# Moving key projections of a context attention beside a selective scan, by way of DRAM

## The chip, the core and the metric

The kernel runs on one core of a Trainium2 chip. The metric is the time of one execution on the device, in microseconds (us); before the change it is 1704.65 us (median of three runs, 1704.19 to 1710.15). The core's engines each work through their own instructions in order: TensorE (PE in the profile; PEld is its weight load), VectorE (DVE), ScalarE (ACT), GpSimd (POOL), and SyncE (SP), which here only issues DMAs. SBUF is the on-chip memory, PSUM the banks that TensorE writes to; DRAM is the memory outside the core.

## The reference, cut to what matters

A residual stream `x` of 4 batches x 128 tokens x 128 channels passes through four layers of three blocks each. Two blocks matter here.

The second block of the first layer is a selective state-space block in two directions, with 256 inner channels and 16 states per channel:

```python
delta = softplus(dt @ dtp_w.T + dtp_b)
A = -exp(A_log)
def step(h, inp):                       # one step in time
    u_t, d_t, b_t, c_t = inp
    h = h * exp(d_t[:, :, None] * A) + (d_t * u_t)[:, :, None] * b_t[:, None, :]
    return h, einsum('bdn,bn->bd', h, c_t)
```

The first block of the second layer is a cross attention of the 128 queries of each batch over 2048 rows of a context `ctx` with 96 channels, with 12 heads of 64 channels, biases on queries, keys and values, and a padding mask:

```python
q = x @ Wq.T + bq; k = ctx @ Wk.T + bk; v = ctx @ Wv.T + bv
weights = softmax(q @ k.T / sqrt(64), masked); out = (weights @ v) @ Wo.T + bo
```

The keys depend on the context and on weights alone, not on `x`, so they can be computed at any time.

## The kernel before, in words

The blocks run one after the other (`BLOCKS`). Weights are loaded with SP one block ahead (`nxt`), into a pool of two buffers. Inside the big blocks the order of the instructions on every engine is the order in which the Python code emits them (`manual_schedule`). A tile is taken from a pool with a fixed number of buffers per tag; an instruction that writes a tile waits until the buffer's last user is done.

**`mamba`, the selective scan.** `project(d)` prepares direction `d` in steps: `inputs` (transposes into `pads`), `conv` (two convolutions `xi_ps`, eight passes each), `gate` (`z_ps`), `dbl` (`xdbl_ps`, the store of the rows of B and C to DRAM as `bc_rows`, then two `dt_ps`), `exps`, `sums`, and `delta` per half (the softplus). All of these take their PSUM banks from the tag `mm`, which has three. Then there are 16 groups `(d, g, half)`: 2 directions x 4 quarters of the states x 2 halves of the channels. For group `i` the loop emits:

- the steps of `project(1)` that `side` puts there (0: inputs, taps; 1: conv, gate; 2: dbl; 3: exps; 4: sums; 5: delta),
- `spread`: SP loads the rows of B and C for the next quarter from DRAM, spread over 128 partitions (`b_rows` L1315, `c_rows` L1317, 1 MB each, two buffers each),
- on DVE the scan of 128 x 2048 (L1372) and the product with C (L1374),
- `total(i - 1)`: on PE eight passes that add up the states of the group before (`y_ps` L1348),
- `inputs(i + 2)`: on ACT four exponentials into `dA` (L1333; two buffers in all, so they wait for scan `i`), on DVE the input of the scan (L1337) into a buffer of the tag `h`, which has four and which `total` frees.

**`ctx_attention(1)` / `attend_units`, the context attention.** The 96 key blocks are 4 batches x 6 groups of two heads x 4 blocks of 512 context rows. A unit is a batch and four heads (two groups), so there are 12 units, three per batch. Per unit there are 8 key blocks (`key_steps`: a matmul `k_ps` L563 from the context, transposed, as `ctxT`; ACT adds the bias and copies to `kT`, L568), 8 score steps (`score_steps`: two matmuls `s_ps` L613 and two DVE instructions L620 that add the mask and take maxima), 8 exponentials (L632), and 16 chunks of four transposes (`t_ps` L726), a copy (`pT`) and the product with the context (`av` L719). The order is written out by hand: key blocks and scores of unit 0, key blocks of unit 1, and then a loop over the units, in which the score steps of the next unit and the key blocks of the one after that are spread over the 16 chunks. `context(b)` loads `ctxT` and `ctx` of a batch with SP; `mask(b)` loads the mask with ACT's queue (`mw` L539) and prepares it on POOL (`maskb` L542). A key fills a `kT` buffer of 128 x 2048; there are three.

Of the kernel before, what the change touches and what calls it, by code (L numbers as in the profile page):

```python
# [9 lines left out]
F32 = mybir.dt.float32  # L10
# [3 lines left out]
AF = mybir.ActivationFunctionType  # L14
# [85 lines left out]
class _XA:  # L100


    def __init__(self, heads, d, values, biases):
        self.heads, self.d = heads, d
        self.rows = 64 if d > 32 else 32
        self.per = P // self.rows
        self.groups = heads // self.per
        self.values = values
        self.biases = biases
        self.at = _Pack()  # L110
        for n, w in [("q", self.groups * P), ("k", self.groups * P), ("v", C if values else self.groups * DC),
                     ("o", heads * C), ("bq", self.groups), ("bk", self.groups), ("bv", self.groups)]:
            self.at.add(n, w)


XA = {1: _XA(12, 64, False, True), 2: _XA(8, 64, False, False), 3: _XA(8, 16, True, True)}


# [16 lines left out]
def _xattn_layout(xa, wq, wk, wv, wo, bq=None, bk=None, bv=None):  # L135

    h, d, g, per, rows = xa.heads, xa.d, xa.groups, xa.per, xa.rows

    def padded(m):
        out = np.zeros((m.shape[0], g, per, rows), np.float32)  # L140
        out[..., :d] = m.reshape(m.shape[0], g, per, d)
        return out.reshape(m.shape[0], g * P)

    def down(m):
        return padded(m.T).T.reshape(g, P, -1).transpose(1, 0, 2)

    out = np.zeros((P, xa.at.width), np.float32)
    out[:, xa.at["q"]] = padded(wq)
    out[:DC, xa.at["k"]] = padded(wk)
    if xa.values:  # L150
        out[:DC, xa.at["v"]] = wv
        out[DC, xa.at["v"]] = bv
    else:
        out[:, xa.at["v"]] = down(wv.T).reshape(P, -1)
    o = np.zeros((per, rows, g, per, C), np.float32)
    wod = down(wo).reshape(per, rows, g, C)
    for j in range(per):
        o[j, :, :, j] = wod[j]
    out[:, xa.at["o"]] = o.reshape(P, -1)
    for n, v in (("bq", bq), ("bk", bk), ("bv", None if xa.values else bv)):  # L160
        if v is not None:
            out[:, xa.at[n]] = down(v[:, None])[:, :, 0]
    return out


def _layout(i):
# [54 lines left out]
        axis=1,  # L221
    )
    a["cwr"] = np.concatenate([w[:, 0].T.reshape(-1) for w in both("conv_w")])[None]
    a["dtp"] = np.concatenate([m.T for m in both("dtp_w")], axis=1)
    a["l0f"] = np.concatenate([i["L0_ffn_w1"], kchunks(i["L0_ffn_w2"])], axis=1)

    a["xa1"] = _xattn_layout(
# [51 lines left out]
class Net:  # L279
    def __init__(self, ctx, tc, A):  # L280
        self.tc, self.nc, self.A = tc, tc.nc, A
        nc = self.nc
        self.cp = ctx.enter_context(tc.tile_pool(name="const", bufs=1))
        self.wp = ctx.enter_context(tc.tile_pool(name="weights", bufs=2))
        self.st = ctx.enter_context(tc.tile_pool(name="stats", bufs=4))
        self.x = self.cp.tile([P, B, C], F32, name="x")
        nc.scalar.dma_start(self.x, A["x"].rearrange("b t c -> t b c"))
        consts = self.cp.tile([P, CONSTS.width], F32, name="consts")
        nc.scalar.dma_start(consts, A["consts"])
        self.k = lambda n: consts[:, CONSTS[n]]  # L290
        self.ident = self.k("ident")
        self.ones = self.cp.tile([P, P], F32, name="ones")
        nc.gpsimd.memset(self.ones, 1.0)
        self.eps = self.cp.tile([P, 4], F32, name="eps")
        nc.gpsimd.memset(self.eps[:, 2:3], -MAGIC)
        nc.gpsimd.memset(self.eps[:, 3:4], EPS * EPS)
        nc.gpsimd.memset(self.eps[:, 0:1], EPS)
        nc.gpsimd.memset(self.eps[:, 1:2], 0.00064)
        cols = self.cp.tile([P, COLS.width], F32, name="cols")
        self.col = lambda n: cols[:, COLS[n]]  # L300
        self._flip = 0
        self._w = {}
        self._rows = {}
        nc.scalar.dma_start(cols, A["cols"])
# [185 lines left out]
    def attend_units(self, es, n, w, qT, wo, sense, first):  # L490
# [26 lines left out]
        def context(b):  # L517
            if b in ctxs or b >= B:
                return ctxs.get(b)
            c = {}  # L520
            lo = b * S + first * P
            c["T"] = cx.tile([DC + 1, keys], F32, tag="cT", name="ctxT")
            nc.sync.dma_start(c["T"][:DC], self.A["ctxT"][:, lo : lo + keys])
            if xa.values:
                nc.gpsimd.memset(c["T"][DC : DC + 1], 1.0)
                c["v"] = cx.tile([P, nch * C + 16], F32, tag="cv", name="val", bufs=1 + ahead)
                nc.gpsimd.memset(c["v"][:, nch * C :], 0.0)
            else:
                c["c"] = cx.tile([P, nch, DC], F32, tag="cc", name="ctx", bufs=1 + ahead)
                nc.sync.dma_start(  # L530
                    c["c"], self.A["ctx"][lo : lo + keys].rearrange("(c p) d -> p c d", p=P))
            ctxs[b] = c
            return c

        def mask(b):
# [8 lines left out]
                    ALU.mult, ALU.add)  # L544
            return masks[b]

        def key_steps(u):

            b, ug = units[u]
# [3 lines left out]

            def key(gi, j):
                def run():
                    c = context(b)
                    if sense is not None and ug == 0 and gi == 0 and j == nkq - 1:
                        mask(b)
                    if j == 0:
                        kT[gi] = kp.tile([P, keys], F32, tag="kT", name="kT")  # L560
                    g = ug * upg + gi
                    ps = s_ps.tile([P, 512], F32, tag="s", name="k_ps")
                    nc.tensor.matmul(  # L563
                        ps, W("k")[:DC, g * P : (g + 1) * P], c["T"][:DC, j * 512 : (j + 1) * 512],
                        start=True, stop=True)
                    to = kT[gi][:, j * 512 : (j + 1) * 512]
                    if xa.biases:
                        nc.scalar.activation(to, ps, AF.Identity, bias=W("bk")[:, g : g + 1])  # L568
                    else:
                        nc.scalar.copy(to, ps)  # L570
                return run

            def val(j):
# [9 lines left out]
                return run  # L583

            for gi in range(upg):
                steps += [key(gi, j) for j in range(nkq)]
            if xa.values and ug == 0:
                steps += [val(j) for j in range(nkq)]
            return steps
# [562 lines left out]
    def mamba(self, nxt):  # L1152
# [4 lines left out]

        nc, tc = self.nc, self.tc
        w = self.load("mamba")
        dtp = self.load("dtp")  # L1160
        MW = 512 + 80 + 256
        G = 4
        nxt()
        with tc.manual_schedule(), ExitStack() as es:
# [6 lines left out]
            xn = one.tile([P, B, C], F32, name="xn")  # L1171
            wc = one.tile([P, 2, 4, 256], F32, name="wc")
            lp = es.enter_context(tc.tile_pool(name="mb3", bufs=2))
            cwr = lp.tile([P, 2, 4, 256], F32, tag="h", name="cwr", bufs=4)
            for d in range(2):
                nc.sync.dma_start(
                    cwr[:, d].rearrange("p k c -> p (k c)"),
# [30 lines left out]
            def project(d):  # L1208
# [73 lines left out]
                def sums():  # L1282
                    for half in range(2):
# [2 lines left out]
                        nc.vector.tensor_scalar(q["r"], s["mm"][half], bias(half), 0.0, ALU.add, ALU.max)  # L1286
                        q["s"] = wk.tile([P, N], F32, tag="sp_s", name="sp_s")
                        nc.vector.tensor_scalar_add(q["s"], q["e"], 1.0)
                        q["l"] = wk.tile([P, N], F32, tag="sp_l", name="sp_l")
                        nc.scalar.activation(q["l"], q["s"], AF.Ln)  # L1290
                    if d == 0:
                        nc.vector.tensor_scalar_mul(A, A, -1.0)

                def delta(half):
                    q = sp[half]
                    nc.vector.scalar_tensor_tensor(q["e"], q["s"], -1.0, q["e"], ALU.add, ALU.subtract)
                    nc.vector.tensor_sub(q["r"], q["r"], q["e"])
                    dl = wk.tile([P, N], F32, tag=f"delta{half}", name="delta")
                    nc.vector.tensor_add(dl, q["r"], q["l"])
                    du = wk.tile([P, N], F32, tag=f"du{half}", name="du")  # L1300
                    nc.vector.tensor_mul(du, dl, s["u"][half])
                    s["delta"].append(dl)
                    s["du"].append(du)
                    s["y"] = []

                return [inputs, conv, gate, dbl, exps, sums, lambda: delta(0), lambda: delta(1)]

            groups = [(d, g, half) for d in range(2) for g in range(G) for half in range(2)]
            rows = {}
# [12 lines left out]
            def inputs(i):  # L1322
# [8 lines left out]
                for n in range(4):  # L1331
# [1 line left out]
                    nc.scalar.activation(  # L1333
                        dA[:, n, :, 1:], s["delta"][half].rearrange("p (b t) -> p b t", b=B)[:, :, 1:],
                        AF.Exp, scale=A[:, c : c + 1])
                dbu = lp.tile([P, 4, N], F32, tag="h", name="h", bufs=4)
                nc.vector.tensor_mul(dbu, bc_mid(s["du"][half], 4), rows[d, g][0])  # L1337
                dbus[i] = dbu

# [25 lines left out]
            for i, (d, g, half) in enumerate(groups):  # L1365
# [10 lines left out]
                if i:  # L1376
                    total(i - 1, hcs.pop(i - 1))
                inputs(i + 2)
            total(len(groups) - 1, hcs.pop(len(groups) - 1))
            out = ops.tile([P, B, C], F32, name="out_ps")  # L1380
            for b in range(B):
# [798 lines left out]
class _Doubled:  # L2180
# [14 lines left out]
    ("ctx_attention", (3, "bo3")), ("causal_attention", ()), ("routed_ffn", ()),  # L2195
]
WEIGHTS = [
    ("l0x",), ("mamba", "dtp"), ("l0f",), ("xa1",), ("r7",), ("moe1",),
    ("xa2",), ("l2a",), ("l2f",), ("xa3",), ("l3a",), ("l3f",),
]  # L2200

# [27 lines left out]
```

## Time and profile before

The profiled execution took 1707.17 us by the clock of the runs; its span, from the first to the last instruction, is 1705.3 us.

| stage | us of the span | what the busy time shows (us of the stage) |
|---|---|---|
| first layer's bit attention, start of the scan block | 0 to 211 | mixed |
| first direction's steps up to the first scan | 211 to 227 | DVE 12.9, ACT 13.2 of 16 |
| the 16 scan groups | 227 to 376 | DVE 146.6, PE 95.9, ACT 47.6 of 149 |
| end of the scan block, grouped feed-forward | 376 to 412 | PE 24.0 of 36 |
| queries of the context attention | 412 to 431 | PE 12.4 of 19 |
| context attention, before its loop | 431 to 465 | mixed |
| context attention, units 0 to 10 and their side work | 465 to 881 | PE nearly without gaps |
| the other eight blocks | 907 to 1705 | not touched but for the third context attention |

The whole execution has PE busy 79% of the span, DVE 58%, ACT 41%, POOL 2%, and the DMA engines move 31 GB/s on the mean. The page and the answers of the trace are read as follows. A line of a group gives line, engine, operation, the tile written and the tiles read; a line in order of time begins with its start and its duration, and what stands in brackets is how long the engine was idle before it and what it waited for. A table by stage gives the length, then the busy time of each engine with the number of instructions, the granted clock of TensorE as a share of its full speed, the share of the DMA engines and GB/s. Matmuls are pipelined, so the shown duration of one is longer than the distance to the next: the distance between two starts is what a pass costs.

### The profile page before, as it was taken

To read this page: it belongs to the slowest core of one execution; us is meant where nothing else is said; L and a number is where in the kernel's file an instruction comes from. 1 tells how busy PE (TensorE), PEld (TensorE's weight loads), DVE (VectorE), ACT (ScalarE), POOL (GpSimd) and SP (SyncE) were. 2 spreads that over 40 slices of the span, in tenths; PEclk is the share of its full clock that TensorE was granted. 3 is DMA by queue.
4 is the path that set the end of the run, shared out by engine and by line. 5 is a ranking of instruction groups with operands and counts; after the bars stand their busy time and mean duration, and the time that the engine had idled before them with its cause. 6 is when DMAs were issued, how large, how long until landed. Compare 5 with 4: busy or idle time off the path is not lost.

```text
span 1705.3 us, 17314 instructions
## 1 busy us (share of the span) xinstructions
PE 1343.3 (79%) x6385; PEld 706.7 (41%) x6387; DVE 991.2 (58%) x2334; ACT 707.6 (41%) x1237; POOL 40.5 (2%) x53
## 2 busy tenths in 40 slices
PE   1478665577799999999995677698968358999987
PEld 0145322234344444444441356473535225455444
DVE  6775499982244445444545877513548644566645
ACT  4653363213544554554432510234524213566642
POOL 0000000000000000000000000000002000000000
PEclk9978777788899999999996775699989556999998
DMA  4000143201300000000100000102000110000010
GB/s 138 0 1 1 30 177 118 98 29 68 80 19 7 19 19 7 19 7 1 42 9 29 1 1 1 50 0 69 18 13 1 48 39 19 20 1 1 2 49 7
DMA packets 21317, 53.57 MB, mean 31 GB/s; under 512 B 12052, under 2 KB 14748, under 8 KB 17000
## 3 DMA queue, kind: packets, MB, share of 16 engines
q1 hardware_dynamic: 17120, 46.55, 8.4%
q10 hardware_dynamic: 4104, 5.82, 1.1%
q8 instruction: 53, 0.87, 0.2%
q14 instruction: 40, 0.33, 0.1%
HBM read 51.97 MB, written 0.39 MB: 31 GB/s over the span
## 4 chain that ended last, share of the span: by engine, by line
PE 60%; DVE 24%; ACT 7%; issue 5%; DMA 2%; POOL 0%; DVEq 0%; ACTq 0%; POOLq 0%; SPq 0%
PE av L719 12%; PE s_ps L613 9%; PE t_ps L726 9%; PE k_ps L563 7%; DVE h L1372 4%; DVE p L620 3%; DVE h L1337 2%; PE av L715 2%; PE h_ps L1932 2%; PE y_ps L1939 2%; PE y L660 1%; PE o_ps L2005 1%; PE s_ps L977 1%; ACT wm L1665 1%; ACT p L632 1%
## 5 line engine op out<-in xcount | busy, mean ns | idle before, releaser
L340 DVE COPY pT<-t_ps 128x512 f32<-128x512 f32 x192 | 132.4, 690 | 219.3 <-PE t_ps L726 207.1
L632 ACT ACTIVATE p<-p,nm 128x1024 f32<-128x1024 f32 (+1 forms) x192 | 206.0, 1073 | 105.2 <-DVE nm L625 105.2
L719 PE MATMUL av<-pT,ctx 128*96 128x512 f32 x448 | 232.3, 606 | 1.0 <-ACT pT L338 1.0
L726 PEld LDWEIGHTS t_ps<-consts,p 128*128 128x128 f32 x1408 | 164.8, 141 | 154.8 <-issue 118.1
L726 PE MATMUL t_ps<-consts,p 128*128 128x128 f32 x1408 | 219.5, 279 | 0.0
L620 DVE CUSTOM_DVE_ANT_0 p<-s_ps,maskb 128x512 f32<-128x512 f32 x224 | 145.2, 688 | 112.1 <-PE s_ps L613 85.7
L338 ACT COPY pT<-t_ps 128x512 f32<-128x512 f32 x192 | 111.8, 582 | 229.7 <-PE t_ps L726 191.8
L613 PE MATMUL s_ps<-kT,qT 64*128 64x512 f32 (+1 forms) x704 | 181.1, 685 | 7.6 <-ACT kT L568 4.8
L563 PE MATMUL k_ps<-ctxT,w_xa 96*128 96x512 f32 x288 | 158.4, 650 | 17.9 <-DMA ctxT<-in_ctxT 14.7
L1348 PE MATMUL y_ps<-h,consts 128*128 128x512 f32 x128 | 80.1, 784 | 51.8 <-DVE h L1374 51.8
L568 ACT ACTIVATE kT<-k_ps,w_xa 128x512 f32<-128x512 f32 x128 | 87.3, 687 | 69.9 <-PE k_ps L563 69.9
L719 PEld LDWEIGHTS av<-pT,ctx 128*96 128x96 f32 x448 | 64.2, 162 | 112.3 <-issue 96.9
L620 DVE CUSTOM_DVE_ANT_0 p<-s_ps,zero 128x512 f32<-128x512 f32 x128 | 80.8, 687 | 37.1 <-PE s_ps L613 37.0
L613 PEld LDWEIGHTS s_ps<-kT,qT 64*128 64x128 f32 (+1 forms) x704 | 58.6, 194 | 44.4 <-issue 15.6
L1333 ACT ACTIVATE dA<-delta,A 128x508 f32<-128x508 f32 x64 | 40.7, 707 | 82.0 <-DVE h L1372 80.4
L1348 PEld LDWEIGHTS y_ps<-h,consts 128*128 128x128 f32 x128 | 30.8, 252 | 100.8 <-DVE h L1374 63.5
L563 PEld LDWEIGHTS k_ps<-ctxT,w_xa 96*128 96x128 f32 x288 | 50.9, 210 | 48.4 <-issue 35.6
L1372 DVE TENSOR_TENSOR_SCAN h<-dA,h 128x2048 f32<-128x2048 f32 x16 | 70.7, 4417 | 0.0
L715 PE MATMUL av<-pT,val 128*32 128x128 f32 x1024 | 55.2, 289 | 13.6 <-DVE pT L340 12.6
L663 DVE SCALAR_TENSOR_TENSOR x<-y,r,x 128x128 f32<-128x128 f32 x112 | 39.3, 351 | 12.8 <-PE y L660 6.5
L715 PEld LDWEIGHTS av<-pT,val 128*32 128x32 f32 x1024 | 20.4, 109 | 63.3 <-DVE pT L340 32.2
L1689 PE MATMUL sap<-pr,consts 128*128 128x64 f32 x120 | 33.3, 380 | 14.4 <-DVE pr L1687 13.7
(518 smaller groups left out, 1806.3 us busy)
## 6 DMA issues: line engine op xcount, KB each, us to landing
ctxT<-in_ctxT SPq DMA_DIRECT2D x12, 768.0 KB, 5.7
b_rows<-bc_rows SPq DMA_DIRECT2D x8, 1024.0 KB, 5.6
c_rows<-bc_rows SPq DMA_DIRECT2D x8, 1024.0 KB, 5.2
w_moe<-in_moe SPq DMA_DIRECT2D x2, 2048.0 KB, 7.4
ctx<-in_ctx SPq DMA_DIRECT2D x4, 768.0 KB, 7.9
w_l3f<-in_l3f SPq DMA_DIRECT2D x1, 1920.0 KB, 7.5
w_xa<-in_xa SPq DMA_DIRECT2D x1, 1833.0 KB, 7.7
w_xa<-in_xa SPq DMA_DIRECT2D x1, 1222.0 KB, 5.3
```

Source lines behind the costliest of these rows:

```text
L338: self.nc.scalar.copy(out, in_)
L340: self.nc.vector.tensor_copy(out, in_)
L563: nc.tensor.matmul(ps, W("k")[:DC, g * P : (g + 1) * P], c["T"][:DC, j * 512 : (j + 1) * 512], start=True, stop=True)
L568: nc.scalar.activation(to, ps, AF.Identity, bias=W("bk")[:, g : g + 1])
L613: nc.tensor.matmul(ps, qT[at, g, b * T : (b + 1) * T], kT[at, j * 512 : (j + 1) * 512], start=True, stop=True)
L620: nc.vector.tensor_tensor_reduce(st["p"][h, j * 512 // hw][:, j * 512 % hw : j * 512 % hw + 512], ps, in1, 1.0, -3.0e38, ALU.add, ALU.max, ...
L632: nc.scalar.activation(t, t, AF.Exp, bias=nm[:, h : h + 1], accum_out=st["s"][:, h, k : k + 1])
L715: nc.tensor.matmul(av[32 * i : 32 * i + 32, 0:P], c["v"][:, ch * C + h * 16 : ch * C + h * 16 + 32], pT[:, i * P : (i + 1) * P], start=ch ...
L719: nc.tensor.matmul(av[:DC], c["c"][:, ch], pT, start=ch == 0, stop=ch == nch - 1)
L726: nc.tensor.transpose(tr[:, i * P : (i + 1) * P], t[:, at : at + P], self.ident)
L1348: nc.tensor.matmul(y, self.ident, hc[:, n], start=g == 0 and n == 0, stop=False)
L1372: nc.vector.tensor_tensor_scan(self.flat(h), dA.rearrange("p n b t -> p (n b t)"), self.flat(h), 0.0, ALU.mult, ALU.add)
```

## The change

60 of the 96 key blocks of the second layer's context attention are projected in the scan's loop. After `inputs(i + 2)` group `i` emits the blocks 60i/16 to 60(i+1)/16: a matmul into a bank of `mm`, an ACT copy into `key` (two buffers), a store with SP into a DRAM tile `keys{b}`. The weights for it (`w_key`, 97 rows) are loaded once with ACT's queue, the context in halves of a batch (`ctx_half`, 97 x 1024, two buffers) with SP, and POOL writes a row of ones. The order of the blocks is batch, half, group, block of the half.

In `key_steps` the function `ready` says how many blocks of a key are there already; if there are any, SP loads them from DRAM into `kT` in one DMA, and their steps are left out. The bias of the keys is now a 97th row of their weights, met by a row of ones below `ctxT`, in the second and the fourth layer; ACT copies without a bias. The tag `h` has three buffers instead of four, the logarithm of the softplus is written in place (with the DVE instruction that reads its argument moved ahead of it), and `dtp` becomes a part of the weights `mamba` (256 KB wider, zeros below its 8 rows).

```diff
+HOISTED = 60
+    if bk is not None:
+        out[DC, xa.at["k"]] = padded(bk[None])[0]
...
+    a["mamba"] = np.concatenate([a["mamba"], np.concatenate([dtp, np.zeros((P - 8, dtp.shape[1]), np.float32)])], axis=1)
...
+            if xa.biases:
+                nc.gpsimd.memset(c["T"][DC : DC + 1], 1.0)
...
+        nk = DC + 1 if xa.biases else DC
+        def ready(b, nkq):
+            return max(0, min(4, 2 * ((HOISTED - b * 48) // 24))) if n == 1 else 0
...
                     if j == 0:
                         kT[gi] = kp.tile([P, keys], F32, tag="kT", name="kT")
+                        if ready(b, nkq):
+                            nc.sync.dma_start(kT[gi][:, : ready(b, nkq) * 512], self.hoisted[b][g, :, : ready(b, nkq) * 512])
+                    if j < ready(b, nkq):
+                        return
+                    c = context(b)
                     ps = s_ps.tile([P, 512], F32, tag="s", name="k_ps")
                     nc.tensor.matmul(
-                        ps, W("k")[:DC, g * P : (g + 1) * P], c["T"][:DC, j * 512 : (j + 1) * 512],
+                        ps, W("k")[:nk, g * P : (g + 1) * P], c["T"][:nk, j * 512 : (j + 1) * 512],
                         start=True, stop=True)
-                    to = kT[gi][:, j * 512 : (j + 1) * 512]
-                    if xa.biases:
-                        nc.scalar.activation(to, ps, AF.Identity, bias=W("bk")[:, g : g + 1])
-                    else:
-                        nc.scalar.copy(to, ps)
+                    nc.scalar.copy(kT[gi][:, j * 512 : (j + 1) * 512], ps)
...
-                steps += [key(gi, j) for j in range(nkq)]
+                steps += [key(gi, j) for j in range(nkq) if j == 0 or j >= ready(b, nkq)]
...
-            cwr = lp.tile([P, 2, 4, 256], F32, tag="h", name="cwr", bufs=4)
+            cwr = lp.tile([P, 2, 4, 256], F32, tag="h", name="cwr", bufs=3)
...
-                        q["l"] = wk.tile([P, N], F32, tag="sp_l", name="sp_l")
-                        nc.scalar.activation(q["l"], q["s"], AF.Ln)
+                        nc.vector.scalar_tensor_tensor(q["e"], q["s"], -1.0, q["e"], ALU.add, ALU.subtract)
+                        nc.scalar.activation(q["s"], q["s"], AF.Ln)
...
+            kp = es.enter_context(tc.tile_pool(name="mb_k", bufs=2))
+            xa = XA[1]
+            wkey = kp.tile([DC + 1, xa.groups * P], F32, name="w_key", bufs=1)
+            nc.scalar.dma_start(wkey, self.A["xa1"][: DC + 1, xa.at["k"]])
+            order = [(b, hf, g, j) for b in range(B) for hf in range(2) for g in range(xa.groups) for j in range(2)]
+            cts = {}
+            def ctx_half(b, hf):
+                if (b, hf) not in cts and order.index((b, hf, 0, 0)) < HOISTED:
+                    t = cts[b, hf] = kp.tile([DC + 1, 1024], F32, tag="ct", name="ctx_half")
+                    lo = b * S + hf * 1024
+                    nc.sync.dma_start(t[:DC], self.A["ctxT"][:, lo : lo + 1024])
+                    nc.gpsimd.memset(t[DC : DC + 1], 1.0)
+            def key(n):
+                b, hf, g, j = order[n]
+                if b not in self.hoisted:
+                    self.hoisted[b] = self.dram.tile([xa.groups, P, S], F32, name=f"keys{b}")
+                ctx_half(b, hf)
+                mm = ps.tile([P, N], F32, tag="mm", name="key_ps")
+                nc.tensor.matmul(
+                    mm, wkey[:, g * P : (g + 1) * P], cts[b, hf][:, j * 512 : (j + 1) * 512], start=True, stop=True)
+                t = kp.tile([P, N], F32, tag="key", name="key", bufs=2)
+                nc.scalar.copy(t, mm)
+                lo = hf * 1024 + j * 512
+                nc.sync.dma_start(self.hoisted[b][g, :, lo : lo + 512], t)
...
                 inputs(i + 2)
+                for n in range(HOISTED * i // 16, HOISTED * (i + 1) // 16):
+                    key(n)
```

## The prediction

> **What bounds the kernel now.** I read the chain of work that ended last first, then the busy time by stage, then the waits and order of time in the two stages that the diff touches.
>
> ```profile
> PE 60%; DVE 24%; ACT 7%; issue 5%; DMA 2%; POOL 0%; DVEq 0%; ACTq 0%; POOLq 0%; SPq 0%
> ```
>
> Busy time by stage (columns named in its first line):
>
> ```profile
> core 0: us, PE busy (x) PEld busy (x) DVE busy (x) ACT busy (x) POOL busy (x), PEclk, DMA share, GB/s
> 227.00:376.00 149.00, 95.86 (x159) 37.27 (x160) 146.57 (x62) 47.60 (x71) 0.00 (x0) 0.80 0.25 92
> 447.00:846.00 399.00, 395.87 (x1540) 184.83 (x1539) 185.53 (x500) 203.50 (x348) 5.70 (x3) 0.99 0.04 10
> ```
>
> Two stages, two limits. The selective scan (227 to 376 us) has DVE busy 146.6 of 149 us: DVE sets its end, PE and ACT have holes. The second layer's context attention (447 to 846) has PE busy 395.9 of 399: every PE pass there is on the path. Work moved from the second to the first pays if it truly fits the holes.
>
> ```profile
> ACT dA L1333 <- DVE h L1372: 80.4, 13, 12.1
> ...
> PE y_ps L1348 <- DVE h L1374: 49.7, 13, 8.4
> ```
>
> Those were the waits of 227 to 372 us (total, times, longest). DVE in order of time (start, duration):
>
> ```profile
> 240.80 2.29 DVE L1374 TENSOR_TENSOR h<-h,c_rows 128x2048 f32<-128x2048 f32 x1
> 243.01 2.28 DVE L1337 TENSOR_TENSOR h<-du,b_rows 128x2048 f32<-128x2048 f32 x1
> 245.21 4.42 DVE L1372 TENSOR_TENSOR_SCAN h<-dA,h 128x2048 f32<-128x2048 f32 x1
> ```
>
> One scan group is three DVE instructions back to back: scan 4.42, product 2.2, next input 2.2 (starts 2.2 apart), 8.86 us in all. ACT's exponentials (4 x 0.64 = 2.55) wait for the scan, PE's sums for the product. In such in-order queues a hole is free only if nothing due stands behind the filler.
>
> The start of the attention and a stretch of its first loop, in order of time:
>
> ```profile
> 437.23 0.33 ACTq L539 DMA_DIRECT2D mw<-in_mask  x1
> 441.29 1.90 POOL L542 TENSOR_SCALAR maskb<-mw 128x2048 bf16<-128x2048 uint8 x1 [35.81 <-DMA mw<-in_mask]
> 443.22 0.69 DVE L620 CUSTOM_DVE_ANT_0 p<-s_ps,maskb 128x512 f32<-128x512 f32 x1 [22.58 <-POOL maskb L542]
> ...
> 479.87 1.02 PE L563 MATMUL k_ps<-ctxT,w_xa 96*128 96x512 f32 x2
> 480.74 1.02 PE L719 MATMUL av<-pT,ctx 128*96 128x512 f32 x2
> ```
>
> In the attention a key block is two passes, 480.74 - 479.87 = 0.87 us of PE. Before its loop (first transposes at 465.16) DVE's first score work waits for the mask, whose DMA stands in ACT's queue behind key copies.
>
> **What the change really moves.** `HOISTED` is 60, and `order` has 24 blocks per batch (2 halves x 6 groups x 2). But `ready` computes 2 * ((60 - 48b) // 24), at most 4: batch 0 gets 4, batch 1 gets 2 * (12 // 24) = 0, later ones 0. So 60 blocks are projected and stored beside the scan, 24 are read, 72 are still projected in the attention, and 36 are done twice. I take this as read off the code.
>
> **Gain in the attention.** Batch 0 is units 0 to 2: 8 blocks each. Unit 2's stand in the loop of unit 0: 8 x 0.87 = 6.9 us of a bound PE. (The last unit, with no side steps at all, still runs PE without gaps at 1.30 us a chunk, so PE stays the limit.) Units 0 and 1 stand before the loop. With no key copies ahead of it, the mask's DMA leaves ACT right after the last query copy (425.93 + 0.69 = 426.6); 4.1 us to Pool's start as now and 1.9 on Pool give 432.7 instead of 443.2. Sixteen score rows at 0.61 and the third of four 1.14 us exponentials then end at 446.4, where unit 1's key blocks now keep PE until 465.16: 18.7 less. Against it stand a PE back at half clock for two chunks (1.5 us), and 1 to 2 us if the mask's 256 KB shares the engines with key loads. The key loads are 1 MB each on SP; a 1 MB row load alone lands in 4.6 us, so 425.96 + 4.6 = 430.6 is before the mask even at the latest start. `ctx` now queues behind four of them: about 448, when the first product needs it. I take 15.5 (13 to 18). Sum 22.4, from 18 to 25. Pool's new 1.8 us memsets have 100 us of idle Pool; copy instead of biased copy (0.59 for 0.69) is off the path.
>
> **Cost in the scan.** Each of 16 groups gets 3 or 4 blocks: two passes (0.43 each at full clock, 0.85 at half, both seen in one sum of eight), an ACT copy (0.59, as ACT's copies of 128x512 take), a 256 KB store on SP. I walked the queues instruction by instruction with these durations; the same walk without keys puts the last scan at 367.1, as the trace does. What came late:
> - Group 1. Three blocks of group 0 hold all three `mm` banks until their copies, which stand behind the exponentials of group 2: scan end 231.9 + 2.55 + 0.59 = 235.1. The second direction's convolution, now at 227.7, waits for that; the sum of group 0 behind it ends near 249.5 instead of 242.3. `h` has three buffers, one fewer, so the input of group 3 (243.0) waits for that sum: 6.5 us of DVE.
> - Group 2. The last copy of group 1 ends at 255.0 (it waits for earlier stores to land); `xdbl`'s copy and its small store come behind it, and SP reaches `b_rows` of the third quarter only at 256.6: it lands 4.6 later, 261.3, and DVE wanted it at 258.3: 3.0.
> - Groups 3 and 4. `dt_ps` holds two banks until `sums` in group 4, so blocks 7 to 14 share one: matmul, copy, matmul, with the sums behind them on PE: 0.3. The last of these stores leaves at 281.7, `b_rows` of the fourth quarter behind it lands at 286.5, DVE wanted it at 283.0: 3.5.
> - Groups 6, 8, 10, 12, where DVE needs the next quarter. The copies begin at scan end + 2.55; the third waits for the first store (two `key` buffers; the kernel's own 256 KB store of `out` took 2.3 us), so the fourth store leaves 7.1 after the scan. `b_rows`, which SP now issues behind it (today as soon as its buffer is free), lands 4.6 later with 0.6 of queue between: 12.3. DVE wants it after product, input, scan and product, 2.2 + 2.2 + 4.4 + 2.2 = 11.1. So 1.2 in groups 10 and 12; 2.1 in group 6, where both row loads wait behind the stores; none in group 8, whose predecessor has a `yT` product (0.7) more.
> - After the last product the last sum (8 passes and 2) stands behind four blocks: 3.3.
>
> Together 6.5 + 3.0 + 0.3 + 3.5 + 2.1 + 2.4 + 3.3 = 21.1, taken as 21. With stores at 1.6 us (the 64 KB store's row) the walk gives 18, with 0.5 us more per loaded MB 25; I keep 15 to 28. The softplus edit moves two 0.68 us DVE steps and removes none: 0. Folding `dtp` into the first weight load adds 256 KB to the start, where the DMA engines are full at about 300 GB/s: 0.7 us (0 to 1).
>
> A rule speaks against the stores: the Trainium skill, DMA: Bandwidth & Descriptors, Anatomy of one DMA, says that about 2 us of every DMA are fixed, mostly the receipt of the last write, longest when the target is HBM. Its fit (2.0 us plus bytes over 436 GB/s) would make an estimated 2.6 us of each store, 0.3 above the row; by it the walk's cost would be about 22 instead of 21.
>
> **Sum.** The profiled execution took 1707.2 us (span 1705.3, 1.9 around it), 2.5 above the median of the runs. 1707.2 + 21 + 0.7 - 22.4 = 1706.5; on the median's scale 1704.0. The walk knows no wait that the code does not show, and such waits only add, so I take 1 more: 1705.
>
> **Rivals.**
> - The row loads fall well behind the key stores (slower). The place is SP's queue: `b_rows` has no slack once the last store of the group before leaves later than 11.1 - 4.6 = 6.5 us after the scan, and every further us is paid by DVE at six row loads. If stores wait for each other (they write one DRAM tile in interleaved rows), the fourth leaves at 3.3 + 3 x 2.3 = 10.2, 3 us later than I took: 6 x 3 = 18 us, 1723; with the early groups longer too, 1730. For it: SP had nothing but loads here, and one wrong wait repeats. Against: the stores write separate bytes.
> - The fillers really hide (faster). PE has 53 us of idle time and ACT 101 in the scan. If the convolution gets its bank in time and row loads are issued early, what is left is the tail of 3.3 and perhaps 3: 1705 - 15 = 1690. Against it: three `mm` banks, and program order on SP.
> - All 60 blocks are used: 36 x 0.87 = 31 us more, 1674. The arithmetic of `ready` excludes it.
>
> **How the numbers follow.** A measurement of this kernel can tell about 0.5%, 8.5 us, from no change. Gain and cost nearly cancel, by bounds from 1705 - 9 to 1705 + 10: chance 0.45, nearly all within 0.5%. Slow row loads 0.32, 1713 to 1730 and over. Hidden fillers 0.22, 1685 to 1696. All 60 used: 0.01. The range reaches to the ends of both neighbours: 1689 to 1730; the likeliest case alone has 1696 to 1715. Faster 0.23, same 0.45, slower 0.32.
>
> **What would show it.** Right: 60 `key` copies and stores in the scan, `k_ps` 48 instructions fewer in the attention, first transposes 15 to 19 us sooner after the last query copy, unit 0's loop 30.5 instead of 37.4 us, the last scan about 18 us later, DVE waiting before L1337's line for a `y_ps` sum early and for `b_rows` in even groups. Wrong: DVE still without gaps in the scan (the second rival), SP waiting for DMA before key stores (the first), or attention units of batch 1 without `k_ps` (the third).

## The result, and the profile after

The changed kernel takes 1720.6 us (median of six runs, 1716.6 to 1725.7) beside 1708.6 us for the kernel before on the same chip: a ratio of 1.0076, 95% interval 1.0052 to 1.0099. It is slower by some 13 us, just past what can be told from no change. The profiled execution has a span of 1720.8 us, 15.5 more than before. All places below are from such profiled executions.

The chain of work that ended last, by engine, on the page after:

```profile
PE 61%; DVE 20%; ACT 8%; issue 4%; DMA 4%; POOL 1%; SPq 0%; DVEq 0%; ACTq 0%; POOLq 0%
```

DVE gave up 4 points and DMA won 2: transfers now stand in the chain. Busy time by stage, the scan first and then the attention's loop:

```profile
core 0: us, PE busy (x) PEld busy (x) DVE busy (x) ACT busy (x) POOL busy (x), PEclk, DMA share, GB/s
232.00:404.00 172.00, 138.53 (x267) 55.67 (x266) 146.61 (x62) 78.32 (x127) 2.84 (x3) 0.85 0.48 168
470.00:862.00 392.00, 386.23 (x1515) 181.61 (x1516) 189.62 (x512) 187.19 (x332) 12.89 (x8) 0.98 0.09 27
```

DVE does the same 147 us of work in the scan, but the stage is 172 instead of 149 us long: DVE now stands idle for 25 us, while PE and ACT are fuller. The holes were filled and the bound engine paid. Its waits between 225 and 412 us:

```profile
engine line waited for: us in total, times, longest us
DVE h L1381 <- DMA b_rows<-bc_rows: 14.5, 5, 4.6
DVE h L1381 <- PE y_ps L1392: 9.4, 2, 6.5
DVE yT L1395 <- PE y_ps L1394: 7.7, 2, 7.0
```

(`yT` is the product with the gate that follows a sum of `y`.) All are new but 4.05 us of the last line. DVE in order of time, the first three groups:

```profile
241.25 4.42 DVE L1416 TENSOR_TENSOR_SCAN h<-dA,h 128x2048 f32<-128x2048 f32 x1
245.70 2.29 DVE L1418 TENSOR_TENSOR h<-h,c_rows 128x2048 f32<-128x2048 f32 x1
254.47 2.29 DVE L1381 TENSOR_TENSOR h<-du,b_rows 128x2048 f32<-128x2048 f32 x1 [6.48 <-PE y_ps L1392]
256.68 4.42 DVE L1416 TENSOR_TENSOR_SCAN h<-dA,h 128x2048 f32<-128x2048 f32 x1
261.13 2.29 DVE L1418 TENSOR_TENSOR h<-h,c_rows 128x2048 f32<-128x2048 f32 x1
268.00 2.29 DVE L1381 TENSOR_TENSOR h<-du,b_rows 128x2048 f32<-128x2048 f32 x1 [4.58 <-DMA b_rows<-bc_rows]
```

What were three instructions back to back now has a wait ahead of each third one: first for a sum of `y` (no free buffer of `h`), then for a row load. Ahead of that sum in PE's queue stands the convolution of the second direction, which has to wait for a bank until ACT has copied a key block out of one:

```profile
239.90 9.38 PE L1239 MATMUL xi_ps<-pad,wc 128*128 128x512 f32 x16 [3.59 <-ACT key L1344]
```

The start of the attention, in order of time:

```profile
464.81 0.34 ACTq L546 DMA_DIRECT2D mw<-in_mask  x1
468.15 1.90 POOL L549 TENSOR_SCALAR maskb<-mw 128x2048 bf16<-128x2048 uint8 x1 [23.94 <-DMA mw<-in_mask]
470.08 0.69 DVE L633 CUSTOM_DVE_ANT_0 p<-s_ps,maskb 128x512 f32<-128x512 f32 x1 [10.64 <-POOL maskb L549]
```

The mask leaves with the last query copy (464.73), and first score work comes 4.7 us after that copy's end instead of 16.6 before. The gain is there. `k_ps` has 48 instructions fewer: 24 blocks are read from DRAM and 60 were written.

Two places were not in the sum. The first is the start. ACT's long sum over `w_l0x` in order of time, before and after:

```profile
17.23 1.06 ACT L831 ACTIVATE junk<-w_l0x 128x1024 f32<-128x1024 f32 x1 [3.58 <-DMA w_l0x<-in_l0x]
```

```profile
21.67 1.06 ACT L844 ACTIVATE junk<-w_l0x 128x1024 f32<-128x1024 f32 x1 [5.17 <-DMA w_l0x<-in_l0x]
```

The second lies between the scan and the feed-forward. The load `ew` of 4 KB holds DVE (in order of time, before and after):

```profile
390.44 0.16 DVE L1405 TENSOR_REDUCE ews<-ew 128x4 f32<-128x8 f32 x1 [6.04 <-DMA ew<-in_ew]
```

```profile
417.12 0.36 DVE L360 BATCH_NORM_AGGREGATE ln_mv<-ln_st 128x2 f32<-128x6 f32 x4
428.66 0.16 DVE L1451 TENSOR_REDUCE ews<-ew 128x4 f32<-128x8 f32 x1 [11.18 <-DMA ew<-in_ew]
```

Its landing took 13.0 us (7.8 before). Three 1 MB key loads and `w_xa` leave SP at 412.3 to 416.8 and share the DMA engines with it; before, it was `w_xa` alone. In the traces' records of single packets, the 512 packets of `ew`, 8 bytes each, take 9.3 us from first to last instead of 3.9. The layer norm behind this reduction in DVE's queue, and so the first feed-forward matmul, wait too.

Where the 16.3 us at the end of the attention (906.62 to 922.96) come from:

| stretch | before | after | change |
|---|---|---|---|
| start to first scan | 227.5 | 232.4 | +4.9 |
| first scan to last `yT` | 151.0 | 179.2 | +28.2 |
| last `yT` to first `h_ps` (`ew`) | 16.6 | 21.8 | +5.2 |
| from there to the load `w_r`, which ends the feed-forward | 16.6 | 17.1 | +0.5 |
| `w_r` to the end of the attention | 494.9 | 472.5 | -22.5 |

### The profile page after: what moved, and what is told of

It is laid out like the page before. It is cut to its first block, busy times and chain, and to the rows that moved or that the text cites. A ratio compares the mean times of both kernels' runs of the same rounds, so it can differ in the third digit from the quotient of the medians.

```text
span 1720.8 us, 17714 instructions
## 1 busy us (share of the span) xinstructions
PE 1367.7 (79%) x6457; PEld 719.5 (42%) x6459; DVE 992.1 (58%) x2334; ACT 716.2 (42%) x1273; POOL 52.4 (3%) x62
## 4 chain that ended last, share of the span: by engine, by line
PE 61%; DVE 20%; ACT 8%; issue 4%; DMA 4%; POOL 1%; SPq 0%; DVEq 0%; ACTq 0%; POOLq 0%
PE av L732 12%; PE s_ps L626 10%; PE t_ps L739 9%; PE k_ps L580 6%; DVE p L633 3%; DVE h L1416 2%; PE av L728 2%; PE h_ps L1978 2%; PE y_ps L1985 2%; DMA b_rows<-bc_rows 1%; PE y_ps L1392 1%; PE y L673 1%; PE o_ps L2051 1%; PE xi_ps L1239 1%; DVE h L1381 1%
## 5 line engine op out<-in xcount | busy, mean ns | idle before, releaser
L580 PE MATMUL k_ps<-ctxT,w_xa 97*128 97x512 f32 (+1 forms) x240 | 130.3, 635 | 9.0 <-DMA ctxT<-in_ctxT 9.0
L583 ACT COPY kT<-k_ps 128x512 f32<-128x512 f32 x120 | 69.9, 585 | 71.4 <-PE k_ps L580 68.0
L1341 PE MATMUL key_ps<-ctx_half,w_key 97*128 97x512 f32 x120 | 64.8, 669 | 37.9 <-ACT key L1344 25.9
L1392 PE MATMUL y_ps<-h,consts 128*128 128x512 f32 x128 | 68.9, 689 | 2.2 <-DVE h L1418 2.2
L1344 ACT COPY key<-key_ps 128x512 f32<-128x512 f32 x60 | 34.1, 582 | 66.3 <-DMA keys<-key 42.1
L1341 PEld LDWEIGHTS key_ps<-ctx_half,w_key 97*128 97x128 f32 x120 | 23.4, 206 | 71.9 <-issue 38.5
L580 PEld LDWEIGHTS k_ps<-ctxT,w_xa 97*128 97x128 f32 (+1 forms) x240 | 40.5, 205 | 27.8 <-issue 21.9
L1381 DVE TENSOR_TENSOR h<-du,b_rows 128x2048 f32<-128x2048 f32 x16 | 36.6, 2288 | 23.9 <-DMA b_rows<-bc_rows 14.5
```

What stands on the lines that cost most here:

```text
L580: nc.tensor.matmul(ps, W("k")[:nk, g * P : (g + 1) * P], c["T"][:nk, j * 512 : (j + 1) * 512], start=True, stop=True)
L1341: nc.tensor.matmul(mm, wkey[:, g * P : (g + 1) * P], cts[b, hf][:, j * 512 : (j + 1) * 512], start=True, stop=True)
L1392: nc.tensor.matmul(y, self.ident, hc[:, n], start=g == 0 and n == 0, stop=False)
```

## The experiments

Each kernel ran beside the kernel before on the same chip, and each ratio is against that; kernels that ran on different chips are compared by their ratios. "Changed" is the changed kernel.

**Count the blocks in twelves**, so that all 60 are read (changed, one line):

```diff
-            return max(0, min(4, 2 * ((HOISTED - b * 48) // 24))) if n == 1 else 0
+            return max(0, min(4, 2 * ((HOISTED - b * 24) // 12))) if n == 1 else 0
```

> The changed kernel with the count in `ready` mended to 2 * ((60 - 24b) // 12), so that all 60 stored blocks are read (batches 0 and 1 whole, half of batch 2). Theory A (PE bounds the attention, a block there is two passes): 36 blocks fewer at 0.87 us, 31 us less than the changed kernel, about 1689 us, 0.989 of the kernel before; the 10 further key loads of 1 or 0.5 MB hide. Theory B (the loop of the attention falls back on key loads, or on DVE and ACT once the side steps are few): less than half of that, 1705 or more.

Measured: 1699.4 us, ratio 0.9934 (0.9910 to 0.9957). So `ready` did throw 36 blocks away, and with them read the change beats the kernel before. The gain over the changed kernel, 24 us by the ratios, lies between the two theories. From the first product to the end of the attention 406.9 us pass instead of 432.5, 25.6 less, not the 31 that 36 x 0.87 makes. By the distances of the units' output products, the three units with no key block at all saved 15.9 of 20.6 us, and three units with half of their blocks 9.7 of 10.3. The busy time of the first two of those units in this kernel, by windows:

```profile
core 0: us, PE busy (x) PEld busy (x) DVE busy (x) ACT busy (x) POOL busy (x), PEclk, DMA share, GB/s
523.00:555.00 32.00, 31.59 (x136) 14.80 (x135) 15.89 (x44) 13.74 (x24) 0.00 (x0) 1.00 0.21 75
555.00:590.00 35.00, 33.45 (x142) 15.87 (x142) 20.09 (x56) 14.12 (x25) 3.70 (x2) 1.00 0.17 61
```

PE has 0.4 and 1.5 us of holes there where it had none; the rest of the missing 5 us stays open.

**Project only the blocks that are read**: 24 projected, 24 read.

```diff
-HOISTED = 60
+HOISTED = 24
-            return max(0, min(4, 2 * ((HOISTED - b * 48) // 24))) if n == 1 else 0
+            return max(0, min(4, 2 * ((HOISTED - b * 24) // 12))) if n == 1 else 0
```

> Only 24 blocks are projected beside the scan, and the same number of blocks is read in the attention as in the changed kernel (here 8 for each of the first three units, counted by twelve). So the attention keeps its gain and only the fillers of the scan change: 24 instead of 60. Theory A (the cost is queueing: what a group can hide costs nothing, and the third and fourth block of a group make nearly all of the wait): first scan to last yT falls from 179.2 us to 153 to 157 (151.0 before the change), time 1694 to 1699. Theory B (each block costs the same, 28.2 / 60 = 0.47 us): 24 blocks cost 11 us, first scan to last yT 162, time about 1704.

Measured: 1696.0 us, ratio 0.9926 (0.9892 to 0.9959). First scan to last `yT` takes 154.0 us, 3.0 more than before the change: theory A. The 36 blocks that nobody reads cost 25 of the 28 us. In the whole scan one wait of DVE for an input is left, in order of time:

```profile
259.30 2.29 DVE L1381 TENSOR_TENSOR h<-du,b_rows 128x2048 f32<-128x2048 f32 x1 [2.01 <-PE y_ps L1392]
```

With three banks, and with the row loads behind the stores, one or two blocks per group fit into the holes; the third and fourth are what DVE pays for. That is no fixed limit: with both of these mended, 60 blocks cost 7.3 us (below, all mends at once).

**Row loads ahead of the key stores** in SP's queue (changed):

```diff
                 inputs(i + 2)
+                if half == 1:
+                    spread(*divmod(d * G + g + 2, G))
                 for n in range(HOISTED * i // 16, HOISTED * (i + 1) // 16):
```

> The changed kernel with the row loads of the next quarter issued one group earlier, ahead of that group's key stores on SP. Theory A (the row loads behind the stores are what DVE waits for): the 14.5 us of DVE waiting for b_rows go, and the time falls by 10 to 15 us, 1706 to 1711. Theory B (ACT and PE are late anyway and take over as the thing waited for): the time falls by less than 4 us.

Measured: 1710.1 us, ratio 1.0007 (0.9993 to 1.0020). First to last scan takes 151.5 us instead of 164.1, and first scan to last `yT` 164.2 instead of 179.2. No wait for `b_rows` is left in the loop; three for sums of `y` are, in order of time:

```profile
255.74 2.29 DVE L1381 TENSOR_TENSOR h<-du,b_rows 128x2048 f32<-128x2048 f32 x1 [6.56 <-PE y_ps L1392]
267.29 2.29 DVE L1381 TENSOR_TENSOR h<-du,b_rows 128x2048 f32<-128x2048 f32 x1 [2.60 <-PE y_ps L1392]
278.73 2.29 DVE L1381 TENSOR_TENSOR h<-du,b_rows 128x2048 f32<-128x2048 f32 x1 [2.49 <-PE y_ps L1392]
```

The order on SP, not the traffic of the stores, made the row loads late: the same 60 stores still run.

**Five `mm` banks** instead of three (changed):

```diff
-            ps = ... tc.tile_pool(name="mb_ps", bufs=3, space=PSUM)
-            yps = ... tc.tile_pool(name="mb_yps", bufs=4, space=PSUM)
+            ps = ... tc.tile_pool(name="mb_ps", bufs=5, space=PSUM)
+            yps = ... tc.tile_pool(name="mb_yps", bufs=2, space=PSUM)
```

> As the changed kernel, but with five `mm` banks of PSUM and two for the sums of y instead of three and four. Theory A (the early waits of DVE, 6.5 us in group 1 and what follows from it in groups 2 to 4, come from key blocks that hold all three `mm` banks until their copies): the 6.5 us wait for y_ps goes, and 8 to 12 us with its followers: 1708.5 to 1712.5. Theory B (the order of ACT's copies and of SP's stores sets these waits, and the banks only pass it on): the waits stay or move to b_rows, less than 4 us: 1717 or more.

Measured: 1712.8 us, ratio 1.0008 (0.9991 to 1.0024); first scan to last `yT` takes 168.9 us, 10.3 less. The size is that of theory A, at the edge of its range, but the wait did not simply go. DVE's waits in this stretch:

```profile
engine line waited for: us in total, times, longest us
DVE h L1381 <- DMA b_rows<-bc_rows: 8.7, 4, 3.7
DVE h L1381 <- PE y_ps L1392: 7.1, 1, 7.1
```

Group 1 has no wait any more and group 2 has one of 7.1 us for a sum of `y`. The banks let the early groups run on until the next shortage: PE then waits 2.3 us for the copy of `xdbl`, which stands on ACT behind four key copies, and these behind key stores. The edit also takes the banks of the sums from four to two; no wait of this stretch is put down to that.

One part of the change was never tried alone: the tag `h` has three buffers instead of four. With a fourth, the input of group 3 would not have to wait for the sum of group 0. So the waits for sums of `y` (9.4 us in the changed kernel) may be in part its price; no run tells.

**`dtp` in the load of the scan weights, alone** (kernel before, with this edit only):

```diff
-    a["dtp"] = np.concatenate([m.T for m in both("dtp_w")], axis=1)
+    dtp = np.concatenate([m.T for m in both("dtp_w")], axis=1)
+    a["mamba"] = np.concatenate([a["mamba"], np.concatenate([dtp, np.zeros((P - 8, dtp.shape[1]), np.float32)])], axis=1)
...
-        dtp = self.load("dtp")
+        dtp = w[:8, 2 * (512 + 80 + 256) :]
```

> The kernel before with one part of the change alone: `dtp` folded into the first weight load (256 KB wider). Theory A (the wider load displaces what the first block waits for): the second sum over the first block's weights starts some 4 us later than in the kernel before, as in the profile of the changed kernel, and the time is 3 to 5 us longer, 1712. Theory B (the 4 us at the start were chance; 256 KB cost what they take to move): under 1 us.

Measured: 1713.0 us, ratio 1.0019 (1.0006 to 1.0032). The long sum starts at 23.14 us (17.23 before), the first scan at 232.85, the attention ends 4.9 us later. The loss at the start is this edit's: in all kernels here that have it, with the weights in one transfer at their old place, the long sum starts at 21.7 to 23.1 us, in those without it at 17.2 to 17.5.

Two kernels ask why 256 KB cost so much. **The scan weights behind all of `ctxT`** (changed):

```diff
         w = self.load("l0x")
-        nxt()
...
                 nc.sync.dma_start(ctxT[:DC, at], self.A["ctxT"][:, at])
+            nxt()
```

> The changed kernel with the first scan weights (w_mamba, now 1,104 KB) loaded on SP's queue behind the four pieces of ctxT instead of behind the first. The same bytes in all. Theory A (bytes that stand ahead: w_l0x on ACT's queue is late because these 1,104 KB are moved before it): the second w_l0x sum, at 21.67 us in the changed kernel and 17.23 before, starts at 17 us or sooner, first scan 228 or sooner, time 4 to 5 us less than the changed kernel. Theory B (the two queues take turns packet by packet, and SP's queue has packets of 8 KB in either order, of ctxT or of the weights): the second sum stays at 20.5 to 23 us, time within 2 us of the changed kernel's.

**The scan weights in four pieces** (changed):

```diff
+            elif name == "mamba":
+                at = self.A[name].shape[1] // 4
+                for j in range(4):
+                    cols = slice(j * at, (j + 1) * at)
+                    self.nc.sync.dma_start(t[:, cols], self.A[name][:, cols])
```

> The changed kernel with the first scan weights loaded in four pieces of 276 KB (2.2 KB per partition row) at the same place of SP's queue. The same bytes in all, smaller packets. Theory B (turns packet by packet): while these pieces move, ACT's queue gets a larger share, and the second w_l0x sum starts at 15 to 18 us instead of 21.67, time 4 to 6 us less than the changed kernel. Theory A (bytes): it stays at 20.5 to 23 us and the time within 2 us of the changed kernel's.

Measured: 1721.0 us, ratio 1.0057 (1.0041 to 1.0074), for the first; 1717.9 us, ratio 1.0052 (1.0034 to 1.0071), for the second. Both intervals overlap that of the changed kernel, so the times do not tell the theories apart; the traces do. The long sum starts at 18.66 in the first, and in the second, in order of time:

```profile
13.76 1.04 ACT L849 ACTIVATE junk<-w_l0x 128x1024 f32<-128x1024 f32 x1
```

So smaller pieces of the same bytes give 7.9 us, past theory B's range, and 3.5 us more than was lost. The later place gives 3.0, which neither theory's range holds. Bytes that stand ahead do not explain it: with all mends (below) the same move takes 848 KB from ahead of `w_l0x`, and the long sum starts later, at 18.60 instead of 17.53.

The traces also record each packet with its queue and size, one per row of a load, and they show what `w_l0x` runs beside. Its own 128 packets (6 KB each) take, from the first start to the last end:

| kernel | `w_l0x` | packets of SP's queue meanwhile |
|---|---|---|
| before | 6.2 us | 122 of `ctxT`, 8 KB each |
| changed | 9.8 us | 209 of `ctxT` |
| `dtp` alone | 11.0 us | 240 of `ctxT` |
| weights later | 6.1 us | 116 of `ctxT` |
| weights in four | 2.7 us | 113 of the weights, 2.2 KB each |

In the changed kernel the weights' packets have ended when those of `w_l0x` begin. So it is not delayed by the wider rows beside it but by what follows them: more of `ctxT` goes beside it. Why 256 KB shift the two queues that far is not shown. The Trainium skill, DMA: Bandwidth & Descriptors, Queues, rings and completion order, states that an engine takes its queues in turn, a whole packet at a time. This agrees with the nearly equal counts in three of the rows (128 beside 113 to 122), not with the 209 and 240.

The end of this stage, when the context's scale is known, moves only from 31.65 to 28.64 and 28.49 us (27.22 before): with the weights in four pieces DVE then waits for `ctxT` instead, 3.8 us. The first scan starts at 225.5 and 225.2 us, 6.9 and 7.2 earlier than in the changed kernel. Only 3 of these come from the stage above; in these two and in the last kernel below, which ran on one chip, the granted clock from 171 to 211 us is 0.74, in all others 0.66 to 0.70.

**`ew` loaded at the start of the scan block**, in the changed kernel and, to see what was there to gain already, in the kernel before:

```diff
+            self.ew = self.cp.tile([P, B, 2], F32, name="ew")
+            nc.scalar.dma_start(self.ew, self.A["ew"].rearrange("(b t) k -> t b k", b=B))
             taps(0)
...
-            ew = one.tile([P, B, 2], F32, name="ew")
-            nc.scalar.dma_start(ew, self.A["ew"].rearrange("(b t) k -> t b k", b=B))
+            ew = self.ew
```

> The changed kernel with the 4 KB load of the expert weights `ew` issued at the start of the scan block instead of after it. Theory A (it lands late, 13 us after its issue, because key loads stand in the same DMA engines, and the feed-forward waits for it): the time from the last `yT` to the first `h_ps` falls from 21.8 to 9 to 12 us, the whole by 9 to 12 us, 1709 to 1712. Theory B (the mask's load, issued just behind it, or the layer norm takes its place): less than 4 us.

> The kernel before with nothing but ew loaded early. It tells how much of the 9.0 us that the same edit won in the changed kernel belongs to the change. Theory A (the small load waited 7.8 us before already, and the change's key loads from DRAM beside it added 5.2): 5 to 7 us faster than before, 1702.5 to 1704.5. Theory B (the wait in the kernel before was hidden by other work, all 9.0 us are the change's): within 1.5 us of before.

Measured: 1711.6 us, ratio 1.0009 (0.9998 to 1.0019) in the changed kernel; last `yT` to first `h_ps` is 10.6 us instead of 21.8. In the kernel before 1705.5 us, ratio 0.9968 (0.9953 to 0.9983); there it is 12.1 instead of 16.6. So 4.5 us were there to gain before the change, as theory A had it, a little under its size. Of the 11.2 us won in the changed kernel, 5.2 are what the change had added (table above); with `ew` early, the stretch is 1.5 us shorter there than in the kernel before, which no run explains.

**All mends at once**: twelves, early rows, early `ew`, five banks, `dtp` by itself; the diffs are those above and the reverse of the one on `dtp`.

> All mends in one kernel: 60 blocks read by counting in twelves, row loads issued ahead of the key stores, ew loaded early, five `mm` banks, and dtp in a load of its own again. Theory A (the costs are separate places and add): 1699.4 - 10.5 (rows) - 9.0 (ew) - 4.9 (start) = 1675, and 0 to 10 less for the banks, which share part of their wait with the rows: 1665 to 1675, some 2 to 2.6% under the kernel before. Theory B (the mends hide one another: with one wait gone the next is due at once): 1680 to 1690.

Measured: 1659.7 us, ratio 0.9702 (0.9664 to 0.9739), 3% faster than the kernel before and better than theory A's range. First scan at 227.42; first scan to last `yT` 158.3 us for 60 blocks. DVE's waits for its inputs in the scan, in order of time:

```profile
244.36 2.29 DVE L1382 TENSOR_TENSOR h<-du,b_rows 128x2048 f32<-128x2048 f32 x1 [1.34 <-PE y_ps L1393]
257.99 2.29 DVE L1382 TENSOR_TENSOR h<-du,b_rows 128x2048 f32<-128x2048 f32 x1 [4.68 <-PE y_ps L1393]
```

By the stretches of the table above, against the changed kernel: 5.0 at the start, 20.9 in the scan, 11.0 at `ew`, 1.0 in the feed-forward and 26.1 from there to the end of the attention, 64.0 in all. The start, `ew` and the blocks read give what they gave alone (4.9 to 5.4, 11.2, and 26.2 over this stretch). The two mends of the scan do not add: alone they gave 15.0 and 10.3 us, together 20.9, so they share 4.4 of their waits.

**The same with the scan weights later**, the edit shown above:

> The kernel with all mends, and its first scan weights (848 KB, without dtp) loaded behind the four pieces of ctxT. Theory A: as the start then has 848 KB less ahead of w_l0x, 2 to 3 us less than the kernel with all mends (1659.7): 1657 to 1658. Theory B: no change of more than 1.5 us, or slower if dtp and the weights then come late.

Measured: 1664.2 us, ratio 0.9734 (0.9711 to 0.9756). No gain beyond the noise, as theory B has it: the two intervals overlap, and the context's scale is known at 28.59 us instead of 27.52. The later place helps only where the wider load has done its damage.

## Why the prediction was right and wrong

The range held the time, but only because it was drawn out to the ends of the rivals; the likeliest case (1696 to 1715) did not hold. No measurable change was forecast, and the kernel is slower. The sum without its last microsecond missed by 17.0 us: 4.2 at the start, 7.2 in the scan, 5.7 at `ew` and the feed-forward, and nothing in the attention. Term by term, in us:

| term | predicted | measured |
|---|---|---|
| start | 0.7 | 4.9 |
| group 1 | 6.5 | 6.5 |
| group 2 | 3.0 | 4.6 |
| groups 3 and 4 | 3.8 | 2.9 |
| groups 6, 8, 10, 12 | 2.1, 0, 1.2, 1.2 | 3.9, 0.6, 3.0, 2.4 |
| behind the last product | 3.3 | 3.6 |
| scan in all | 21 | 28 |
| `ew` and the feed-forward | not seen | 5.7 |
| attention up to its first product | -15.5 | -16.8 |
| the rest of it (loop of unit 0) | -6.9 | -5.7 |

- **The reading of the code was right.** 24 of 60 blocks are read; the kernels with twelves and with 24 blocks show both sides of it.
- **The attention was right**: 22.5 us for 22.4. The first transposes come even 24 us sooner after the last query copy, not 15 to 19, but then stand twice for ACT's exponentials (2.42 and 1.94 us).
- **The mechanism of the scan was right, its size a quarter too small.** The five-bank kernel and the kernel with early rows bear out the two waits named, banks held by key blocks and row loads behind stores. The row loads were mis-sized: 14.5 us of waits where the walk made 11.0. `b_rows` took 5.3 to 6.8 us to land in the groups that waited longest, where the walk took the 4.6 of a load alone. In group 2 that is all of it: the load left SP 28.8 us after the first scan's start, as in the walk (29.1). In groups 6, 10 and 12 it also left SP late, 9.7, 8.6 and 8.1 us after the scan instead of 7.7, because the key copies waited longer for stores (2.70 and 1.45 us in group 6). A store took 2.5 us in the median, 2.3 in the walk. The fit of the Trainium skill that the prediction quotes (DMA: Bandwidth & Descriptors, Anatomy of one DMA, where it stands for DMAs that GpSimd issues) makes an estimated 2.6, which is near. Group 3's wait for a sum, 2.9 us, came instead of group 4's wait for rows.
- **The start was wrong by 4.2 us.** The step was to price 256 KB by the mean rate of full DMA engines (at 300 GB/s that is 0.87 us, not the 0.7 taken). The last packet of SP's loads did end only 1.6 us later, but the transfer that the next step needs is on the other queue, and its landing moved 4.4 us. The price is to be read where somebody waits, not at the end of the traffic.
- **`ew` was missed, 5.2 us.** The prediction gave the new key loads a time and asked who waits for them; it did not ask which other load they would sit beside. A load with a wait of 7.8 us stood in the trace of before at just that place.
- **The single microsecond for unseen waits was the weakest step.** The text says that such waits only add, and then takes 1; `ew` and the feed-forward alone made 5.7. With gain and cost nearly equal, each of the three misses was enough to decide the sign.
- **The rivals.** "The row loads fall well behind the key stores" has the sign and, with 1713 to 1730, the time, and its mechanism is there. But it priced that mechanism at 18 us above the sum and got 3.5; its time came out by luck, from the start, `ew` and the rest of the scan. "The fillers really hide" is false for 60 blocks here and nearly true for 24 (3.0 us); where its conditions were met, a bank in time and early row loads, 60 blocks cost 7.3 us, near its 6.3. "All 60 used" is what the kernel with twelves became, at 25.6 instead of 31 us.

## What to carry to other kernels

Work that is moved into an engine's holes does not cost in proportion: one or two fillers per step cost 3 us in all here, three or four cost 28, because in-order queues hand each delay to the engine that sets the pace. The depth is not fixed: with two more banks and the row loads ahead of the stores, three or four cost 7.3. Before moving work, count in the code how much of it is read again, and put the loads that the bound engine needs next ahead of the new stores in their queue. Ask of every new or widened transfer which small load with a reader waiting is in flight beside it.

## What the hardware showed that was not expected

- The same 1,104 KB on one queue delayed a 768 KB load on another queue by 7.9 us more in one transfer than in four. Beside the load's own 128 packets ran 209 packets of 8 KB in the first case and 113 of 2.2 KB in the second.
- A load of 4 KB took 7.8 us beside a load of 1.8 MB, and 13.0 us beside that and 3 MB of key loads. It is moved in 512 packets of 8 bytes.
- The granted clock in the scan rose when PE had more to do there: 0.85 instead of 0.80, and a pass of the sums of `y` took 689 ns in the mean instead of 784. From 250 to 370 us it is 0.77 in the kernel before, 0.84 with 24 blocks, 0.89 in the changed kernel and 0.90 with all mends, where PE is busy for 70, 83, 94 and 103 of the 120 us. Part of what the fillers cost PE came back so.
